# L1 slots and attention's norms emitted in steps, with blocks in between

## Chip, cores and metric

The kernel runs on one core of a Trainium2 chip. The metric is the device time of one launch in microseconds (us). All arithmetic is in 32-bit floats.

## The reference, cut to what matters

2048 tokens of 256 features (two sequences of 1024, seen by the layer-1 attention as they stand) go through two "macaron" layers: half an expert layer, a mixing layer, half an expert layer.

```python
x = x + 0.5 * _L0_ffn_ref(_layernorm(x), ...)   # 8 experts of width 176, top 2, and a shared expert
x = x + _L0_attn_ref(_layernorm(x), ...)        # RWKV time mix and channel mix
x = x + 0.5 * _L0_ffn_ref(_layernorm(x), ...)
x = x + 0.5 * _L1_ffn_ref(_layernorm(x), ...)   # 32 experts of width 96, top 6, and a shared expert
x = x + _L1_attn_ref(_layernorm(x), ...)        # linear attention with rotary turns, no softmax
x = x + 0.5 * _L1_ffn_ref(_layernorm(x), ...)

def _L1_ffn_ref(hidden_states, gate_w, wg, wu, wd, sg, su, sd):
    scores = jax.nn.sigmoid(x @ gate_w)
    topk_w, topk_i = jax.lax.top_k(scores, TOP_K)
    topk_w = topk_w / (jnp.sum(topk_w, axis=-1, keepdims=True) + 1e-20)
    ...
    routed = jnp.einsum('tef,efd,te->td', act, wd, combine)
    shared = jax.nn.silu(hidden_states @ sg) * (hidden_states @ su) @ sd
    return routed + shared

def _L1_attn_ref(X, W_in, b_in, W_out, b_out):
    Q, K, V = jnp.split(jnp.einsum('bsd,ed->bse', X, W_in) + b_in, 3, axis=-1)
    A = jnp.sum(feature_map(K) * V, axis=-2)      # K and Q turned before
    return jnp.einsum('bsd,ed->bse', A[:, None, :] * Q, W_out) + b_out + X
```

## The kernel before

**Names.** The tokens are 16 tiles of 128 in `x`, which stays on the chip. Four tiles are a group (`BT`). Layer 0's second expert layer is `L_0` or m0 (all 16 tiles, four groups); layer 1's are done in passes 0 and 1, each in halves A and B of 8 tiles, so `L_0A`, `L_0B`, `L_1A`, `L_1B`, each with groups g0 and g1. In the profile's names the numbers of groups and buffers are left out.

**An expert layer.** For each group, `measure` normalizes the rows (`normalize`, lines 129 to 147: statistics and the norm on VectorE, a square root and part of the norm on ScalarE, into `xn`, or `axl_at` in pass 1), turns them over on TensorE (psum `pt`, line 156), copies them back on ScalarE (`xT`, line 442), and multiplies them with the router (`lg`, line 456). `choose` finds the top six on VectorE (`taken`, line 202, and the weights). `plan` counts the chosen rows per expert (`count`, line 479), ranks them (`rank`, line 501 ff., and `far`, line 528) and gives each its row number in a table sorted by expert (`idx`, line 567). `scatter` writes the rows to that table in HBM with indirect transfers from GpSimd (`xs_A`, `xs_B`, line 576). Measure, choose and plan together are called the slots of a group.

**Blocks.** The sorted table is worked in blocks of 128 rows (78 for m0; at least 68 and up to 79 for each half of layer 1). A block loads its rows (`xb`), transposes them (`px`, line 755, copied to `xbT` on ScalarE), multiplies with its expert's gate and up weights (`pg`, line 777; `g` on ScalarE, `h` on VectorE), transposes h (`ph`, line 687), multiplies with the down weights (`py`, line 794), copies to `yb` on VectorE (line 802) and stores to `ys`. `combine` gathers each token's six rows (`yk`, indirect transfers from GpSimd, line 814) and adds them into `x` on VectorE (line 826). The shared expert is done by the tile, with the same psum tags. Blocks past the sure number stand behind a condition on the counts (line 919).

**Attention** (`attend`, once per half between the passes): `norms` of a group, then a tile at a time (`tile_of`), then the sum A, and `out_of`, whose products `po` (line 1021) are added into `x` at line 1270. Then follow the slots of pass 1.

**What sets the order.** Each engine does its instructions in the order in which they were emitted, as a scheduler keeps it. `Clock` (line 307) is a planner written by hand: each block runs with `clock.run(us)` for a planned time (`BLOCK`, 2.45 us in layer 0, 1.41 in layer 1), and within it wakes threads that are due: gathers, scatters, slots, attention. `yield clock.spent(us, gap)` says that the part just emitted takes `us` of the blocks' engine time, and is due again `gap` later. What a thread emits under `behind_blocks()` is pinned behind the newest block's last product and yb copy. GpSimd's transfers have one fixed order (`in_turn`), three and then a pause of five memsets; those of `between()` are in one written order: gathers of m0 for groups 0 and 1, scatters of 0A g0, gathers of m0 g2, scatters of 0A g1, gathers of m0 g3, scatters of 0B.

**Where the change lies.** `onward` emits the slots of an L1 group among the blocks of the stage before: first `prep` (measure and choose) in one piece, then `plan` in one. `attend` emits a group's `norms` in one piece, due again after 8.0 us. The slots of 0A and 0B g0 lie among m0's last blocks, those of 0B g1 at the first blocks of 0A, those of 1A among the last of 0B, those of 1B at the end of 0B's shared tiles and the first blocks of 1A.

Of the kernel before, what the change touches and what calls it, by code (L numbers as in the profile page):

```python
# [55 lines left out]
def macaron_kernel(ctx: ExitStack, tc: tile.TileContext, a: dict, out: bass.AP):  # L56
# [12 lines left out]
    def bank(tag, name):  # L69
        return psum.tile([P, TB], F32, tag=tag, name=name)  # L70
# [53 lines left out]
    def statistics(src, n, name):  # L124

        mv = small.tile([P, n, 2], F32, tag="mv", name=f"mv_{name}", bufs=4)
        for i in range(n):
            st = small.tile([P, 6], F32, tag="st", name=f"st_{name}_{i}", bufs=4)
            nc.vector.bn_stats(st, src[i])
            nc.vector.bn_aggr(mv[:, i, :], st)  # L130
        rstd = small.tile([P, n], F32, tag="rstd", name=f"rstd_{name}", bufs=4)
        nc.scalar.activation(rstd, mv[:, :, 1], AF.Sqrt, bias=eps)
        nc.vector.reciprocal(rstd, rstd)
        shift = small.tile([P, n], F32, tag="shift", name=f"shift_{name}", bufs=4)
        nc.vector.scalar_tensor_tensor(shift, mv[:, :, 0], -1.0, rstd, ALU.mult, ALU.mult)
        return rstd, shift

    def normalize(src, dst, n, name):

        rstd, shift = statistics(src, n, name)  # L140
        for i in range(n):
            if i % 2:
                nc.scalar.activation(
                    dst[i], src[i], AF.Identity, bias=shift[:, i : i + 1], scale=rstd[:, i : i + 1]
                )
            else:
                nc.vector.tensor_scalar(
                    dst[i], src[i], rstd[:, i : i + 1], shift[:, i : i + 1], ALU.mult, ALU.add
                )
        return rstd, shift  # L150

    def transposed(src, c, name):

        pt = bank("pt", f"pt_{name}_{c}")
        for i in range(BT):
            nc.tensor.transpose(
                pt[:, i * P : (i + 1) * P], src[i][:, c * P : (c + 1) * P], ident
            )
        return pt
# [216 lines left out]
    clock = Clock()  # L376
# [11 lines left out]
    @contextmanager  # L388
    def behind_blocks():
        with ExitStack() as st:  # L390
            for d in clock.block.values():
                st.enter_context(tc.issue_after(d))
            yield
# [7 lines left out]
    def sparse_moe(layer, w, name, x, xs, ys, moe, given=None, out=None, bufs=2, counts="pt"):  # L401
# [25 lines left out]
        def places(t):  # L427

            h, i = divmod(t, HT)
            if h not in xn:  # L430
                pool = home["pool"]
                xn[h] = pool.tile([P, HT, D], F32, tag="xn", name=f"xn_{name}_{h}", bufs=2)
                xT[h] = pool.tile([P, DC, SEQ], F32, tag="xT", name=f"xTs_{name}_{h}", bufs=2)
            return xn[h], xT[h], i
# [3 lines left out]
        def features_of(b, xb, xbT, o, sub):  # L438

            normalize(x[BT * b : BT * b + BT], xb, BT, sub)  # L440
            for c in range(DC):
                nc.scalar.copy(xbT[:, c, o * P : o * P + TB], transposed(xb, c, sub))

        logits = {}

        def measure(b):
            sub = f"{name}_{b}"
            xb, xbT, o = places(BT * b)
            xb = [xb[:, o + i, :] for i in range(BT)]
            sent[b] = xb  # L450
            features_of(b, xb, xbT, o, sub)
            lg = bank("pt", f"lg_{sub}")[:, 0 : BT * E].rearrange("p (t e) -> p t e", e=E)
            logits[b] = lg
            for i in range(BT):
                for c in range(DC):
                    nc.tensor.matmul(
                        lg[:, i, :],
                        xbT[:, c, (o + i) * P : (o + i + 1) * P],
                        w["router"][:, c, :],
                        start=(c == 0),  # L460
                        stop=(c == DC - 1),
                    )

        def choose(b):
            ts = slice(BT * b, BT * b + BT)
            route(w, logits.pop(b), f"{name}_{b}", taken[:, ts, :], comb[:, ts, :])

        def prep(b):
            measure(b)
            choose(b)  # L470

        def plan(g):


            sub = f"{name}_{g}"
# [21 lines left out]

            pr = bank("py", f"rank_{sub}")[:, 0 : BT * E].rearrange("p (t e) -> p t e", e=E)  # L500
            nc.tensor.matmul(pr, before, taken[:, lo:hi, :], start=True, stop=False)
            for t in range(BT - 1):
# [63 lines left out]
                nc.vector.max(top[:, t, :], slot[:, t, :])  # L566
            nc.vector.tensor_scalar(idx[:, lo:hi, :], top[:, lo:hi, 0:K], -1.0, None, ALU.add)
            groups.append(dict(count=count, cum=cum, open=open_))

        def scatter(g, rank=0):  # L570

            for t in range(BT * g, BT * g + BT):
                for k in range(K):
                    yield from clock.call(rank)
                    with in_turn():
                        d = nc.gpsimd.indirect_dma_start(  # L576
                            out=xs,
                            out_offset=bass.IndirectOffsetOnAxis(
                                ap=idx[:, t, k : k + 1], axis=0
                            ),  # L580
                            in_=sent[g][t - BT * g],
                            in_offset=None,
                        )
                    clock.called(d)
                    tc.declare_no_dep(
                        d.ins, group=f"slots_{name}", reason="a slot is one pair's"
                    )
                    tc.add_to_no_dep_group(f"slots_{name}", d.ins)
                    scattered.append(d.ins)
# [58 lines left out]
        parts = [0] * NT  # L648
# [241 lines left out]
        def blocks(onward=None):  # L890
# [34 lines left out]
        return dict(  # L925
            home=home,
            measure=measure,
            choose=choose,
            prep=prep,
            plan=plan,  # L930
            scatter=scatter,
            owners=owners,
            weights=weights,
# [213 lines left out]
    def wait(done):  # L1147
        while not done():
            yield clock.now + 1.0

    def attend(s, moe, added, result):
# [9 lines left out]
        def norms(g):  # L1161
            ts = slice(g * BT, (g + 1) * BT)
            lg = [xl[:, t, :] for t in range(TPB)][ts]
            rstd, minus[g] = normalize(xs[ts], lg, BT, f"{name}_{g}")
            for c in range(DC):
                nc.scalar.copy(
                    xT[:, c, g * TB : (g + 1) * TB], transposed(lg, c, f"{name}_{g}")
                )

            more = small.tile([P, BT], F32, tag="more", name=f"more_{name}_{g}")  # L1170
            nc.vector.tensor_scalar(more, rstd, 1.0, None, ALU.add)
            for i, xt in enumerate(xs[ts]):
                nc.vector.scalar_tensor_tensor(
                    xt, xt, more[:, i : i + 1], at["b_out"], ALU.mult, ALU.add
                )
# [54 lines left out]

        for g in range(TPB // BT):
            yield from wait(lambda: g in added)
            with behind_blocks():
                norms(g)
            yield clock.now + 8.0
            for t in range(g * BT, (g + 1) * BT):
                with behind_blocks():
                    tile_of(t)
                yield clock.spent(3.0, 4.6)
# [68 lines left out]

    def slots_of(b):
        def slots():  # L1310
            m0["prep"](b)
            m0["plan"](b)
            every_step(m0["scatter"](b))

        return slots
# [9 lines left out]
    def every_step(part):  # L1325
        clock.pool = 0.0
        for _ in part:
            clock.pool = 0.0
# [48 lines left out]
    with ExitStack() as rwkv_stack:  # L1377
# [3 lines left out]
        with tc.tile_pool(name="moe_L0_0", bufs=1) as pool:  # L1381
            m = sparse_moe("L0", w0, "L0_0", x, xs["L0"], ys["L0"], pool, bufs=1, counts="py")
# [24 lines left out]
        for h in range(2):  # L1407
# [7 lines left out]
        rw["pool"] = rwkv_stack.enter_context(tc.tile_pool(name="rwkv", bufs=1))  # L1415
        early_pool = l0_stack.enter_context(tc.tile_pool(name="early", bufs=1, side="right"))
        m0 = sparse_moe(
            "L0",
            w0,
            "L0_1",  # L1420
            x,
            xs["L0"],
            ys["L0"],
            early_pool,
            bufs=1,
# [21 lines left out]
    def half(n, h, **more):  # L1447
# [2 lines left out]
            "L1", w1, f"L1_{n}{k}", x[HT * h : HT * h + HT], xs[k], ys[k], moe_pool, **more  # L1450
        )

    def onward(m, g, planned):

        with behind_blocks():
            m["prep"](g)
        yield clock.spent(6.0, 12.0)

        if g == 0:
            yield from wait(lambda: not planning)  # L1460
            planning.append(m)
        with behind_blocks():
            m["plan"](g)
        yield clock.spent(3.5, 7.0)
        planned.add(g)
        if g == m["groups"] - 1:
            planning.pop()
# [154 lines left out]
```

## Time and profile before

| | |
|---|---|
| runs | 1374.47, 1380.77, 1383.33 us, median 1380.77 |
| profiled execution | 1382.64 us, span 1380.9 us, mean granted TensorE clock 0.913 |
| TensorE busy | 1243.8 us, 90% of the span |
| weight loads, VectorE, ScalarE, GpSimd busy | 965.4, 710.3, 610.7, 660.5 us |
| first L1 slot to the end of 1A's start (562 to 1110 us), TensorE idle in gaps over 0.4 us | 55.8 us |
| GpSimd, indirect transfers | gathers and scatters, about 0.97 us each |

How to read the lines: PE is TensorE, PEld its weight loads, DVE VectorE, ACT ScalarE, POOL GpSimd, SP SyncE. A line of a timeline gives the start in us from the span's start, the length in us, engine, line of the kernel, operation, what it writes and reads, shapes and how many instructions were joined (x8); in square brackets is the idle time of the engine just before, and what ended it. The page's digits are 40 slices of the span, each the busy share in tenths (9 is 90% or more); PEclk is the clock that TensorE was granted, in tenths of full speed.

### The profile page before, as it was taken

The numbers are of one execution on the slowest core, as the hardware profiler recorded it, in microseconds if no ns is written. First come the engines' busy times: TensorE is split into PE (matmuls) and PEld (weight loads), VectorE is DVE, ScalarE is ACT, GpSimd is POOL, SyncE is SP. The second block draws the span as 40 slices with busy tenths as digits, with TensorE's granted clock in tenths as the row PEclk, the third lists the DMA queues.
The fourth block names the chain that finished last, engine by engine and source line by source line (L and its number), as shares of the span: only waits on it lengthen the run. The fifth ranks groups of instructions, "written<-read, shape, count | busy, mean of one in ns | idle before, by whom it ended". The sixth has DMA issues, their size and how long they took to land. (4 is left out here: it accounts for less than half of the span.)

```text
span 1380.9 us, 23073 instructions
## 1 busy us (share of the span) xinstructions
PE 1243.8 (90%) x6100; PEld 965.4 (70%) x6100; DVE 710.3 (51%) x2500; ACT 610.7 (44%) x1660; POOL 660.5 (48%) x1296
## 2 busy tenths in 40 slices
PE   7999999899998899899799998988899789999970
PEld 5767765566676677677579986867655679989850
DVE  5432567644414423554454456764587345456653
ACT  4324475865524133533245555543323155556520
POOL 0620443111113702577777175406667777276475
PEclk9799999999997699999879999997889699999995
DMA  9813434980009224432948685623322258788743
GB/s 284 266 65 108 144 101 133 307 288 1 0 0 243 81 89 126 123 111 92 265 163 269 199 236 175 193 74 103 104 66 77 80 193 265 215 248 265 236 134 105
DMA packets 195171, 214.94 MB, mean 156 GB/s; under 512 B 40893, under 2 KB 178013, under 8 KB 195037
## 3 DMA queue, kind: packets, MB, share of 16 engines
q1 hardware_dynamic: 170460, 146.22, 34.3%
q0 software_dynamic: 24576, 67.14, 15.8%
q8 instruction: 59, 0.97, 0.3%
q14 instruction: 76, 0.61, 0.2%
HBM read 103.04 MB, written 110.23 MB: 154 GB/s over the span
## 5 line engine op out<-in xcount | busy, mean ns | idle before, releaser
L814 POOL DMA_INDIRECT yk_L<-ys_L,idx_L x64 | 61.8, 965 | 174.5 <-DMA ys_L<-yb_L 120.0
L333 POOL MEMSET still<- 128x96 f32 x588 | 105.3, 179 | 33.7
L777 PE MATMUL pg_L_b<-L0gu,xbT_L 128*128 x312 | 108.1, 470 | 1.0 <-ACT xbT_L L759 0.6
L576 POOL DMA_INDIRECT xs_L<-xn_L,idx_L x64 | 61.8, 966 | 78.3 <-DVE taken_L L202 31.4
L670 PE MATMUL pg_L<-L0sgu,xTs_L 128*128 128x352 f32 x256 | 97.7, 516 | 1.7 <-DVE h_L L660 1.3
L814 POOL DMA_INDIRECT yk_L_0B<-ys_B,idx_L_0B x48 | 49.2, 1026 | 72.1 <-DMA xb_L_0B<-xs_B 46.9
L794 PE MATMUL py_L_b<-L0down,hT_L_b 88*128 x312 | 81.3, 382 | 0.0
L814 POOL DMA_INDIRECT yk_L_0A<-ys_A,idx_L_0A x48 | 46.3, 965 | 60.9 <-DMA xb_L_0A<-xs_A 28.7
L660 DVE TENSOR_TENSOR h_L_b<-g_L_b,pg_L_b 128x176 f32<-128x176 f32 x78 | 26.2, 336 | 92.1 <-ACT g_L_b L659 78.8
L794 PEld LDWEIGHTS py_L_b<-L0down,hT_L_b 88*128 88x128 f32 x312 | 58.9, 192 | 19.1 <-issue 0.8
L814 POOL DMA_INDIRECT yk_L_1A<-ys_A,idx_L_1A x48 | 46.8, 975 | 48.0 <-DMA xb_L_1A<-xs_A 23.9
L777 PEld LDWEIGHTS pg_L_b<-L0gu,xbT_L 128*128 128x128 f32 x312 | 55.2, 195 | 20.5 <-DVE h_L_b L660 1.3
L670 PEld LDWEIGHTS pg_L<-L0sgu,xTs_L 128*128 128x128 f32 x256 | 50.6, 212 | 25.5 <-issue 5.9
L777 PE MATMUL pg_L_0B_b<-L1gu,xbT_L_0B 128*128 x272 | 60.8, 351 | 1.3 <-DVEq L919 1.3
L1009 PE MATMUL pkk_cm<-mk_cm,w_WkeyT 128*128 128x512 f32 x128 | 58.7, 594 | 1.5 <-ACT sk_cm L1110 0.9
L777 PE MATMUL pg_L_0A_b<-L1gu,xbT_L_0A 128*128 x272 | 59.3, 343 | 0.8 <-DVE h_L_0A_b L660 0.4
L1021 PE MATMUL pkv_cm<-w_WvalT,sk_cm 128*128 128x256 f32 x256 | 58.6, 379 | 0.1
L814 POOL DMA_INDIRECT yk_L_1B<-ys_B,idx_L_1B x48 | 45.7, 951 | 26.9 <-DMA ys_B<-yb_L_1B 11.7
L1021 PEld LDWEIGHTS pkv_cm<-w_WvalT,sk_cm 128*128 128x128 f32 x256 | 48.3, 190 | 13.7 <-issue 7.2
L777 PE MATMUL pg_L_1A_b<-L1gu,xbT_L_1A 128*128 x272 | 57.3, 334 | 0.3 <-DVE m_L_1B L193 0.2
L777 PE MATMUL pg_L_1B_b<-L1gu,xbT_L_1B 128*128 x272 | 55.7, 327 | 1.3 <-DVEq L919 1.3
L576 POOL DMA_INDIRECT xs_A<-xn_L_0A,idx_L_0A x48 | 46.8, 975 | 18.4 <-issue 13.1
(640 smaller groups left out, 3306.0 us busy)
## 6 DMA issues: line engine op xcount, KB each, us to landing
xs_A<-zero SPq DMA_DIRECT2D x1, 10112.0 KB
xs_B<-zero SPq DMA_DIRECT2D x1, 10112.0 KB
xb_L<-xs_L SPq DMA_DIRECT2D x78, 128.0 KB
ys_L<-yb_L SPq DMA_DIRECT2D x78, 128.0 KB
xb_L_0A<-xs_A SPq DMA_DIRECT2D x68, 128.0 KB
ys_A<-yb_L_0A SPq DMA_DIRECT2D x68, 128.0 KB
xb_L_0B<-xs_B SPq DMA_DIRECT2D x68, 128.0 KB
ys_B<-yb_L_0B SPq DMA_DIRECT2D x68, 128.0 KB
```

Source lines behind the costliest of these rows:

```text
L333: d = nc.gpsimd.memset(still, 0.0)
L576: d = nc.gpsimd.indirect_dma_start(out=xs, out_offset=bass.IndirectOffsetOnAxis(ap=idx[:, t, k : k + 1], axis=0), in_=sent[g][t - BT * g], ...
L660: nc.vector.tensor_tensor(dst, g, pg[:, width : 2 * width], ALU.mult)
L670: nc.tensor.matmul(pg, xbT[:, c, i * P : (i + 1) * P], w["sgu"][:, c, u, :, :].rearrange("p z w -> p (z w)"), start=(c == 0), stop=(c == D ...
L777: nc.tensor.matmul(pg, xbT[:, c, :], w["gu"][:, c, bass.ds(e, 1), :, :].rearrange("p e z h -> p (e z h)"), start=(c == 0), stop=(c == DC - 1),
L794: mm = nc.tensor.matmul(py, hT[0:HP, k, :], w["down"][:, bass.ds(e, 1), k, :].rearrange("p e d -> p (e d)"), start=(k == 0), stop=(k == C ...
L814: d = nc.gpsimd.indirect_dma_start(out=yk, out_offset=None, in_=ys[0 : n * P, :], in_offset=bass.IndirectOffsetOnAxis(ap=idx[:, t, k : k + ...
L1009: nc.tensor.matmul(ps, w[:, c, oc * P : (oc + 1) * P], src[:, c, :], start=(c == 0), stop=(c == DC - 1),)
L1021: nc.tensor.matmul(ps, src[:, c, i * P : (i + 1) * P], w[:, c, :], start=(c == 0), stop=(c == n - 1),)
```

## The change

A slot of layer 1 is emitted in four pieces instead of two: norms; transposes, logits and choice; counts; ranks. Attention's norms are emitted in two pieces: the norm itself; transposes and the rest. Each piece is pinned behind the newest block (`in_steps`, `behind_blocks`). The planned times of a slot sum to the same as before, 6.0 and 3.5 us, with gaps of 12 and 7 us, and 8.0 us for the norms. The slots of layer 0 (`slots_of`) keep their order.

```diff
--- before.py
+++ after.py
@@ -438,17 +438,22 @@
         def features_of(b, xb, xbT, o, sub):
 
             normalize(x[BT * b : BT * b + BT], xb, BT, sub)
+            yield 1.5, 5.5
             for c in range(DC):
                 nc.scalar.copy(xbT[:, c, o * P : o * P + TB], transposed(xb, c, sub))
 
         logits = {}
 
         def measure(b):
+            for _ in measure_steps(b):
+                pass
+
+        def measure_steps(b):
             sub = f"{name}_{b}"
             xb, xbT, o = places(BT * b)
             xb = [xb[:, o + i, :] for i in range(BT)]
             sent[b] = xb
-            features_of(b, xb, xbT, o, sub)
+            yield from features_of(b, xb, xbT, o, sub)
             lg = bank("pt", f"lg_{sub}")[:, 0 : BT * E].rearrange("p (t e) -> p t e", e=E)
             logits[b] = lg
             for i in range(BT):
@@ -465,11 +470,16 @@
             ts = slice(BT * b, BT * b + BT)
             route(w, logits.pop(b), f"{name}_{b}", taken[:, ts, :], comb[:, ts, :])
 
-        def prep(b):
-            measure(b)
+        def prep_steps(b):
+            yield from measure_steps(b)
             choose(b)
+            yield 4.5, 6.5
 
         def plan(g):
+            for _ in plan_steps(g):
+                pass
+
+        def plan_steps(g):
 
 
             sub = f"{name}_{g}"
@@ -497,6 +507,7 @@
 
 
 
+            yield 1.5, 2.0
             pr = bank("py", f"rank_{sub}")[:, 0 : BT * E].rearrange("p (t e) -> p t e", e=E)
             nc.tensor.matmul(pr, before, taken[:, lo:hi, :], start=True, stop=False)
             for t in range(BT - 1):
@@ -566,6 +577,7 @@
                 nc.vector.max(top[:, t, :], slot[:, t, :])
             nc.vector.tensor_scalar(idx[:, lo:hi, :], top[:, lo:hi, 0:K], -1.0, None, ALU.add)
             groups.append(dict(count=count, cum=cum, open=open_))
+            yield 2.0, 5.0
 
         def scatter(g, rank=0):
 
@@ -926,8 +938,9 @@
             home=home,
             measure=measure,
             choose=choose,
-            prep=prep,
+            prep_steps=prep_steps,
             plan=plan,
+            plan_steps=plan_steps,
             scatter=scatter,
             owners=owners,
             weights=weights,
@@ -1162,6 +1175,7 @@
             ts = slice(g * BT, (g + 1) * BT)
             lg = [xl[:, t, :] for t in range(TPB)][ts]
             rstd, minus[g] = normalize(xs[ts], lg, BT, f"{name}_{g}")
+            yield
             for c in range(DC):
                 nc.scalar.copy(
                     xT[:, c, g * TB : (g + 1) * TB], transposed(lg, c, f"{name}_{g}")
@@ -1230,9 +1244,13 @@
 
         for g in range(TPB // BT):
             yield from wait(lambda: g in added)
+            parts = norms(g)
             with behind_blocks():
-                norms(g)
-            yield clock.now + 8.0
+                next(parts)
+            yield clock.now + 5.5
+            with behind_blocks():
+                next(parts, None)
+            yield clock.now + 2.5
             for t in range(g * BT, (g + 1) * BT):
                 with behind_blocks():
                     tile_of(t)
@@ -1308,7 +1326,8 @@
 
     def slots_of(b):
         def slots():
-            m0["prep"](b)
+            m0["measure"](b)
+            m0["choose"](b)
             m0["plan"](b)
             every_step(m0["scatter"](b))
 
@@ -1450,18 +1469,23 @@
             "L1", w1, f"L1_{n}{k}", x[HT * h : HT * h + HT], xs[k], ys[k], moe_pool, **more
         )
 
+    def in_steps(parts):
+
+        while True:
+            with behind_blocks():
+                cost = next(parts, None)
+            if cost is None:
+                break
+            yield clock.spent(*cost)
+
     def onward(m, g, planned):
 
-        with behind_blocks():
-            m["prep"](g)
-        yield clock.spent(6.0, 12.0)
+        yield from in_steps(m["prep_steps"](g))
 
         if g == 0:
             yield from wait(lambda: not planning)
             planning.append(m)
-        with behind_blocks():
-            m["plan"](g)
-        yield clock.spent(3.5, 7.0)
+        yield from in_steps(m["plan_steps"](g))
         planned.add(g)
         if g == m["groups"] - 1:
             planning.pop()
```

## The prediction

> **What bounds the kernel now.** I read the page first, then the PE timeline from 540 to 1115 us with the idle time ahead of each instruction, then POOL's, DVE's and ACT's timelines around each place that the change touches, and last the chain of waits. The page says that TensorE is the bound, with one light stretch in slices 17 to 32:
>
> ```profile
> PE 1243.8 (90%) x6100; PEld 965.4 (70%) x6100; DVE 710.3 (51%) x2500; ACT 610.7 (44%) x1660; POOL 660.5 (48%) x1296
> PE   7999999899998899899799998988899789999970
> POOL 0620443111113702577777175406667777276475
> PEclk9799999999997699999879999997889699999995
> ```
>
> A slice is 34.5 us. Where PE falls to 7 or 8, PEclk falls too. The L1 slots and attention's norms lie there. The PE timeline shows one such place (slots of 1A, first and second group):
>
> ```profile
> 948.43 0.70 PE L794 MATMUL py_L_0B_b<-L1down,hT_L_0B_b 96*128 x2
> 954.96 1.97 PE L156 MATMUL pt_L_1A<-ident,axl_at 128*128 128x128 f32 x8 [5.83 <-DVE axl_at L147]
> 957.39 3.69 PE L456 MATMUL lg_L_1A<-L1router,axT_at 128*128 128x32 f32 x16 [0.46 <-ACT axT_at L442]
> 960.89 1.01 PE L687 MATMUL ph_L_0B_b<-ident,h_L_0B_b 128*96 128x128 f32 x2
> ...
> 967.43 0.41 PE L479 MATMUL count_L_1A<-ones,taken_L_1A 128*32 128x1 f32 x8
> ...
> 988.67 1.97 PE L156 MATMUL pt_L_1A<-ident,axl_at 128*128 128x128 f32 x8 [3.60 <-DVE axl_at L147]
> ```
>
> PE stands still until the norm is done, transposes, takes the logits, and then has 6.5 us of block work (960.89 to 967.43) before the counts. So today the transposes wait and the counts don't. The same waits ahead of transposes elsewhere: 0A g0 1.68 + 0.66 us (562.6), 0A g1 0.87 + 1.45 (584.6), attention of pass 0 2.08 (841.9) and 3.37 (898.4), 1A g0 5.83 + 0.46, 1A g1 3.60 + 0.46, attention of pass 1 1.52 (1050.4), 1B g0 2.44. They sum to 24.4 us: the most that direct waiting can give back.
>
> The second bound is POOL, which moves all rows of the routed experts in one order fixed by hand:
>
> ```profile
> 573.85 0.95 POOL L814 DMA_INDIRECT yk_L<-ys_L,idx_L  x1 [0.30 <-issue]
> 581.24 1.01 POOL L576 DMA_INDIRECT xs_A<-xn_L_0A,idx_L_0A  x1 [5.31 <-DVE idx_L_0A L567]
> ...
> 1000.27 0.97 POOL L814 DMA_INDIRECT yk_L_0B<-ys_B,idx_L_0B  x1 [4.68 <-DVE x L721]
> ```
>
> After 581.24 POOL has no gap until 764, and from 936.6 to 1106 it waits only 4.68 us and less than 5 more. Pass 1A begins at 1109.52 after a PE wait of 4.96 us for rows that POOL's last scatter (1104.87) brought. So between 936 and 1109 a PE wait counts only if it holds up a POOL transfer.
>
> **The change, part by part.** The same matrix products, copies and transfers are issued; the planned time is the same too (1.5 + 4.5 = 6.0 and 1.5 + 2.0 = 3.5 us of blocks per slot, 5.5 + 2.5 = 8.0 per norm). Only the order moves, and two activation table loads are added. Nothing ahead of the first L1 slot (562 us) changes, nor the tail after 1324.
>
> *Transposes behind a block.* About one block (1.45 us in L1, 2.45 in L0) now runs on PE between norm and transposes. Gain: up to that much of each wait.
>
> *Counts lose their cover.* Blocks that stood between logits and counts now stand before the transposes. By the new order, 0A keeps only a px, 0B g1 nothing, 1A g0 a ph and a pg pair, 1A g1 and 1B g1 a few small products. The bare way from logits to counts is in the trace where nothing covers it: at 1B g0 lg ends at 1092.35 and the counts start at 1094.49, 2.14 us. I price the new waits at 2.2, 2.2, 2.2, 1.3, 1.2 and 0.7 us for 0A g0, 0A g1, 0B g1, 1A g0, 1A g1, 1B g1: +9.8 us in all on PE. Hiding them would take 2.2 us of block work that the new order does not offer.
>
> *DVE's order.* Splitting lets the gathers' adds of x (L826) in front of the slot's small operations, and DVE waits there for the landing:
>
> ```profile
> 953.89 0.48 DVE L826 SCALAR_TENSOR_TENSOR x<-yk_L_0B,wk_L_0B,x 128x256 f32<-128x256 f32 x1 [1.55 <-DMA yk_L_0B<-ys_B,idx_L_0B]
> 954.48 0.74 DVE L147 TENSOR_SCALAR axl_at<-x,rstd_L_1A,shift_L_1A 128x256 f32<-128x256 f32 x2
> ...
> 957.35 0.95 POOL L814 DMA_INDIRECT yk_L_0B<-ys_B,idx_L_0B  x1 [0.30 <-issue]
> ```
>
> Before, the norm's last step stands behind the add of a gather issued at 950.5. After, for 1A g0, three more adds stand ahead of it, among them that of the gather of 957.35, which lands some 3 us later: transposes at about 961.4 instead of 954.96. The moved blocks fill 4.9 of these 6.4 us, so the wait becomes about 7.4 instead of 5.83. With 1.3 at the counts the slot numbers come near 974.5, where POOL wants them at 973.9 (the scatter moves ahead of one gather): +0.6 on POOL. At 0A g0, the adds of the gathers of 571 to 574 stand ahead of the choice (before: behind it), the counts come near 577 instead of 575.69, and the numbers near 584.9 instead of 580.96: POOL's first scatter is 3.9 us later.
>
> *Sums by place.* (1) 0A and 0B slots. Everything on POOL up to 764 is 3.9 us late. Rows of 0A are not needed before 682, some 3 us after that, and SyncE holds the loads back for other tables anyway (PE waits of 6.10 and 2.79 us at 674.7 and 682.8). But the last gather of L0 delays the add at 688.66, thus 0B g1's transposes (693.41) by 3.9. PE fills this with the shared ph and py and one pg pair, 4.0 us, that stood behind the logits; then the counts wait 2.2. Counts before at 701.31; after 697.3 + 1.15 + 0.6 + 2.23 + 2.2, near 703.6 to 704: +2.7. The PE gains at 0A g0 (2.3) vanish into the 2.2 at its counts, and so at g1 (2.3 against 2.2). Ends: −4.7 (waits vanish, POOL on time) and +6.1 (3.9 + 2.2, nothing fills). I take +2.7.
>
> (2) Attention of pass 0. These waits lie ahead of 936.59, where POOL's full stretch begins, so they count whole. g0 gets 4 us of block work ahead of its transposes, but ACT puts a table load, a g and an xbT copy (1.28 + 0.25 + 0.37) ahead of its share of the norm; g1's square root stands behind another block's g, its last step behind a yb copy. I take 0.75 each: −1.5; ends 0 and −5.45 (both waits gone).
>
> (3) 1A slots and the end of 0B. In the new order 0B's last block stands ahead of 1A g1's transposes: its end comes 6.4 us earlier, 990.3. POOL still has 12 scatters queued, which end at 996.5: its 4.68 us at 1000.27 shrink by 3.8. Ends: −4.7 (wait gone) and +6 (numbers of 1A g0 late by the whole 6.4, POOL waits with everything behind it). I take −3.8 + 0.6 = −3.2.
>
> (4) Attention of pass 1 on PE: some +2.9 us (two table loads and a g on ACT ahead of the copies), covered by the 4.96 us wait at 1104.57; without that cover it would be paid. I take 0.
>
> (5) 1B g1 among PE-bound blocks: +0.7; ends 0 and +2.2.
>
> *Table loads.* The row, with what follows on ACT:
>
> ```profile
> 841.42 1.28 ACT L132 ACT_TABLE_LOAD   x1
> 842.72 0.30 ACT L132 ACTIVATE rstd_at<-mv_at,eps 128x4 f32<-128x4 f32 x1
> ```
>
> Two more cost ACT 2.6 us, inside (4). The Trainium skill ("ScalarE: Activation LUTs", What ACT_TABLE_LOAD costs) speaks against interleaving other functions: it counts a switch at about 2.66 us, 1283 ns of load and as much again of drain. The 1283 agree with this row, the drain does not show here, since the next ACTIVATE starts 0.02 us after the load; by the page the two would cost 5.3 us and (4) might show through at the 1A start, by the row they stay under it.
>
> *Clock.* In the window 949 to 972, which starts with the 5.83 us wait, the granted clock is 0.70, and 0.85 in 563 to 570 after waits of 1.68 and 0.66. Waits of 2 us in all were thus enough before; I keep the clock as it is and leave its change to the range. The Trainium skill ("TensorE: Matmul & The Clock Gate", Part 1) puts the throttle at an idle window of about 3.4 us; by it the places with 2.2 us would run at full clock, which would give a few us more. The row at 563 does not agree.
>
> Sum: 2.7 − 1.5 − 3.2 + 0 + 0.7 = −1.3, rounded with half-clock pieces that get shorter at 1A g1 to −2 us. The profiled execution took 1382.64 us, span 1380.9 and 1.7 around it; the median of the runs, 1380.77, lies 1.9 below. Set against the median: 1379 us.
>
> **The rivals.** (a) *Waits vanish.* The moved blocks cover the norms, counts are hidden by what DVE finishes sooner. For it: each norm chain is short, and 46.87 us of POOL idle before 936.59 would carry a gain on. Against: the 2.14 us at 1092.35. −4.7 (0A) −5.45 (attention) −4.7 (POOL at 1000): −14.8, about 1366 us. Chance 0.19.
>
> (b) *POOL late.* Adds of x ahead of the slot's operations on DVE make the numbers late, and POOL, in order, holds every later transfer. For it: the 5.31 us wait at 581.24 is of this kind. Against: POOL's 4.68 us at 1000.27 can absorb as much. Price 6.1 in (1) and 6 in (3), with 0.7: +13, about 1394 us. It decides once the 1A g0 numbers come over 5 us after 973.9. Chance 0.20.
>
> (c) *The change does not do what it says.* With planned time unchanged, waits only change name, transposes to counts, place by place: 0 to +1, 1381 us. Chance 0.11. It differs from the forecast in 0B's end, which stays at 1000.
>
> **How the numbers follow.** The forecast, 1379, has 0.50; its own range is 1373 to 1386 (ends of (2), half of those of (1) and (3)). The range 1364 to 1393 reaches to (a) and (b). One per cent is 13.8 us, about what a measurement can tell from no change: below 1367 lies 0.18 (most of (a)), above 1394.6 lies 0.18 (half of (b) and unknown clock loss), between them 0.64.
>
> **What would show it.** Right: idle time of 1 to 2.5 us "<-DVE taken" ahead of the counts at 0A, 0B g1 and 1A; 5 to 8 us still ahead of 1A g0's transposes; the first 0A scatter some 4 us later after its gathers; POOL's wait at the end of 0B under 2 us; the 1A start within 5 us of 1109. Wrong: no count waits (a), or a POOL wait over 5 us for 1A's numbers (b), or PE idle between 540 and 1110 away from its 56 us by more than 8.

## The result and the profile after

The changed kernel takes 1392.32 us (median of 20 runs, 1382.46 to 1398.85), the kernel before 1380.09 us (20 runs, 1370.76 to 1390.97). The ratio is 1.0081, with a 95% interval of 1.0056 to 1.0105: slower by 0.8%, some 11 us. The profiled execution has a span of 1391.0 us and a mean granted clock of 0.908.

From the page of the changed kernel, the same four lines as before:

```profile
PE 1244.7 (89%) x6100; PEld 966.2 (69%) x6100; DVE 711.8 (51%) x2500; ACT 617.8 (44%) x1662; POOL 664.1 (48%) x1296
PE   7999999899997899799789999987998799999970
POOL 1520534111114603377777175407777777166475
PEclk9899999999997699899879999996889589999995
```

PE's busy time is nearly the same in sum (1244.7 us against 1243.8), so most of the 10 us more of span is time in which it waited; within single stages the busy time moves with the clock, as shown below. In the PEclk line four slices are lower by a tenth (from 556, 939, 1078 and 1113 us on), and the second is higher by one.

To see where the time went, I took the start of the same instruction in both traces and subtracted the shift that the two have where their order is still equal (product 231 of layer 0's blocks, 548.2 us before, 546.1 after: −2.1 us, which belongs to the execution and not to the change).

| start of | before | later after the change, shift taken off | of it in this stage | forecast |
|---|---|---|---|---|
| last product of layer 0's shared expert | 655.4 | +9.0 | +9.0 | |
| 131st block transpose of 0A | 794.0 | +12.6 | +3.6 | +2.7 for both |
| 17th product of attention's `pqk` | 910.2 | +2.8 | −9.8 | |
| POOL's first gather of 0B | 936.6 | +6.3 | +3.5 | −1.5 for both |
| first block transpose of 1A | 1109.5 | +5.1 | −1.2 | −3.2 |
| 131st block transpose of 1A | 1209.1 | +9.5 | +4.4 | +0.7 |
| end | 1380.9 | +12.3 | +2.8 | 0 |

The last column is the prediction's term for the stage.

The loss is at 0A's slots. PE's timeline there, and 60 us later among the shared products:

```profile
568.59 0.42 PE L767 MATMUL px_L<-ident,xb_L 128*128 128x128 f32 x2
576.16 0.58 PE L489 MATMUL count_L_0A<-ones,taken_L_0A 128*32 128x1 f32 x8 [7.16 <-DVE taken_L_0A L202]
...
638.58 0.94 PE L699 MATMUL ph_L<-ident,h_L 128*128 128x128 f32 x3 [2.99 <-DVE h_L L672]
```

The waits ahead of 0A g0's transposes are gone (they were 1.68 and 0.66 us), and one of 7.16 us stands ahead of its counts. DVE's timeline says what `taken`, the result of the choice, waited for:

```profile
573.34 0.48 DVE L838 SCALAR_TENSOR_TENSOR x<-yk_L,wk_L,x 128x256 f32<-128x256 f32 x1 [1.27 <-DMA yk_L<-ys_L,idx_L]
573.75 0.46 DVE L193 MAX8 m_L_0A<-s_L_0A 128x8 f32<-128x32 f32 x4
...
575.88 0.23 DVE L202 TENSOR_SCALAR taken_L_0A<-rest_L_0A 128x128 f32<-128x128 f32 x1
...
636.45 0.48 DVE L838 SCALAR_TENSOR_TENSOR x<-yk_L,wk_L,x 128x256 f32<-128x256 f32 x1 [8.09 <-DMA yk_L<-ys_L,idx_L]
```

The logits end at 568.75. Six adds of x, each waiting for a gather to land, stand on DVE between 564.5 and 573.8 ahead of the choice (MAX8); before, it was one. So `taken` ends 7.4 us after the logits; before, it was 2.5. POOL's timeline shows the numbers' lateness:

```profile
587.44 1.01 POOL L588 DMA_INDIRECT xs_A<-xn_L_0A,idx_L_0A  x1 [12.16 <-DVE idx_L_0A L578]
```

The first scatter starts at 587.44, 8.3 us later than before when the shift is taken off (the prediction had 3.9). It holds up the gathers behind it: at 636.45 an add on DVE waits 8.09 us for one of them, an `h` stands behind the add, and PE waits 2.99 us for that `h`. The windows give the clock, 546 to 627 (layer 0's blocks with 0A's slots) and 852 to 870 (attention's first norm) of the changed kernel:

```profile
546.00:627.00 81.00, 71.17 (x351) 53.49 (x350) 43.52 (x174) 33.95 (x81) 47.23 (x101) 0.89 0.35 113
...
852.00:870.00 18.00, 15.36 (x73) 10.83 (x73) 14.10 (x43) 9.54 (x28) 8.13 (x17) 1.00 0.45 142
```

and the one that answers to the second, before:

```profile
842.00:860.00 18.00, 14.92 (x59) 10.96 (x60) 10.68 (x35) 8.98 (x24) 5.00 (x12) 0.81 0.41 130
```

The number after the five engines is the granted clock. At attention it rose from 0.81 to 1.00. The norms' waits there on PE are shorter (2.08 and 3.37 us before):

```profile
855.58 0.44 PE L156 MATMUL pt_at<-ident,axl_at 128*128 128x128 f32 x2 [1.14 <-ACT axl_at L143]
...
907.92 1.09 PE L156 MATMUL pt_at<-ident,axl_at 128*128 128x128 f32 x8 [1.38 <-DVE axl_at L147]
```

At 1A g0 the wait is longer, as forecast:

```profile
965.42 1.97 PE L156 MATMUL pt_L_1A<-ident,axl_at 128*128 128x128 f32 x8 [7.92 <-DVE axl_at L147]
```

### The profile page after: what moved, and what is told of

It is laid out like the page before. It is cut to its first block, busy times and chain, and to the rows that moved or that the text cites. A ratio compares the mean times of both kernels' runs of the same rounds, so it can differ in the third digit from the quotient of the medians.

```text
span 1391.0 us, 23120 instructions
## 1 busy us (share of the span) xinstructions
PE 1244.7 (89%) x6100; PEld 966.2 (69%) x6100; DVE 711.8 (51%) x2500; ACT 617.8 (44%) x1662; POOL 664.1 (48%) x1296
## 5 line engine op out<-in xcount | busy, mean ns | idle before, releaser
L789 PE MATMUL pg_L_0B_b<-L1gu,xbT_L_0B 128*128 x272 | 57.2, 335 | 1.2 <-DVEq L931 0.7
```

The source lines that it names most:

```text
L789: nc.tensor.matmul(pg, xbT[:, c, :], w["gu"][:, c, bass.ds(e, 1), :, :].rearrange("p e z h -> p (e z h)"), start=(c == 0), stop=(c == DC - 1),
```

## The experiments

Theory A: at 0A's first slot the adds of x get ahead of the choice on DVE; the choice comes late, and with it PE's counts and POOL's scatters. Theory B: the counts lost the blocks that covered them, at all six places alike. Theory C: chance in the granted clock. The kernels ran on several chips, on which the kernel before takes 1380 to 1420 us, so ratios to the kernel before on the same chip are compared, each with its 95% interval, and positions in the traces only relative to the shift named above. A trace is one execution; runs of one kernel scatter with a standard deviation of some 5 us, the furthest 10 us from the median.

### Which slots

The change taken apart: a slot that isn't in steps is emitted as before.

```diff
-        yield from in_steps(m["prep_steps"](g))
+        stepped = f"{m['name']}" in SPLIT or f"{m['name']}_{g}" in SPLIT
+        if stepped:
+            yield from in_steps(m["prep_steps"](g))
+        else:
+            with behind_blocks():
+                for _ in m["prep_steps"](g):
+                    pass
+            yield clock.spent(6.0, 12.0)
```

(and in the same way for `plan_steps`; `SPLIT` lists the halves in steps). All in steps but 0A:

> Only the two slots of 0A are put back into one piece each (6.0 and 3.5 us of planned time, as before the change); all else stays split. Theory A (0A's first slot: the adds of x get ahead of its choice on DVE, POOL's scatters start late, and the lateness travels to 0A's start): this kernel loses the delay at 562 to 716 us and keeps what attention gains, so 1374 to 1380 us against 1380 of before, some 12 us under the changed kernel. Theory B (the counts lost their cover at all six places alike): only two of six places are mended, so about 1388. Theory C (chance in the granted clock): 1390 as the changed kernel.

Only 0A, attention's norms whole:

> The kernel before with only the two slots of 0A emitted in steps; the other slots and attention's norms in one piece. Theory A: the whole delay up to 716 us appears here, +9 to +13 us, so 1389 to 1393 us, with 0A's first block some 9 us later than before and everything after it shifted evenly. Theory B: two of the six count waits, +3, about 1383. Theory C: within 3 us of before.

Only attention's norms:

> Attention's norms in two pieces, all slots in one piece as before. Nothing before 836 us moves. Theory A: the gain of some 5 us that the trace of the changed kernel shows between 840 and 860 us stays, of which POOL's full stretch passes on most: 1375 to 1378 us, a little faster than before. Theory B says nothing on it, the prediction's own term was -1.5: 1379. Were attention's split a loss, it would be over 1382.

All slots, attention's norms whole:

> All L1 slots in steps, attention's norms in one piece. Theory A: the changed kernel without its one gain, 1394 to 1398 us. Theory B: about 1391. If the norms' split were itself a part of the loss, it would come out under 1390.

| kernel | ratio | interval |
|---|---|---|
| all but 0A | 1.0026 | 0.9997 to 1.0056 |
| only 0A | 1.0097 | 1.0062 to 1.0132 |
| only attention's norms | 0.9977 | 0.9946 to 1.0008 |
| all slots, norms whole | 1.0074 | 1.0045 to 1.0103 |

0A's two slots alone cost as much as the whole change. Theory A's place is right; theory C had the kernel with only 0A within 3 us of before, and it is 16 us above. Theory A's sizes were less good: all but 0A was expected at 0.996 to 1.000 and came out at 1.0026 (its interval reaches just under 1), so the other slots may cost a little, and all slots with the norms whole was expected at 1.010 to 1.013 and came out at 1.0074, where theory B had put it (1391 us, 1.008). So in these times the norms' split gains little. Alone it gains 0.2%, not clear of its interval, though both traces with it show PE some 9 to 10 us sooner between 844 and 910 us and neither without it does. In the kernel with only 0A the wait is nearly the same:

```profile
584.60 0.59 PE L489 MATMUL count_L_0A<-ones,taken_L_0A 128*32 128x1 f32 x8 [6.53 <-DVE taken_L_0A L202]
```

and its window over layer 0's last blocks, the same work as 548 to 626 before (78 us at a clock of 0.91):

```profile
555.00:642.00 87.00, 77.80 (x349) 57.45 (x348) 44.17 (x174) 33.77 (x80) 50.86 (x109) 0.80 0.34 108
```

### Which split, and whether the adds are the cause

Only the second half of 0A's slots in two pieces (counts, ranks):

> The kernel before, but the slots of 0A have only their second half (counts, ranks) in two pieces; norm to choice stay one piece. In DVE's order the choice then still stands behind one add of x, as before. Theory A (adds of x ahead of the choice): ratio to before 1.000, within 0.3%, no count wait over 1 us. Rival B2 (pinning the ranks behind a block of 2.45 us delays the slot numbers): POOL's first scatter 2.5 to 5 us late and about +0.5%.

Only the first half in pieces:

> The kernel before, with the slots of 0A split in front of the transposes and behind the choice, and the counts and ranks in one piece. Five adds of x stand ahead of the choice, as the norm's split makes it. Theory A: nearly the whole loss of the 0A split, ratio 1.007 to 1.010, a count wait of 4 us or more at 0A g0. Rival B2 (the ranks' pinning): 1.003 or less.

0A as in the change, but the adds of x for m0's group 1 emitted later:

```diff
-        def combine(g, rank=0, lag=4):
+        def combine(g, rank=0, lag=4, flush=0.8):
...
-                yield clock.now + 0.8
+                yield clock.now + flush
...
-        yield from given_rows(m0, (0, 1), added0)
+        yield from given_rows(m0, (0,), added0)
+        yield from wait(lambda: 1 in m0["ready"])
+        yield clock.now + 3.0
+        yield from m0["combine"](1, 0, 7, 2.4)
+        added0.add(1)
```

> The slots of 0A in steps exactly as in the kernel with only 0A split (ratio 1.0097), but the adds of x for m0's group 1 are emitted later (eight gathers ahead of the first add instead of five, 2.4 us between the last ones), so that two adds instead of six stand ahead of the choice on DVE. Theory A: the wait at 0A g0's counts falls from 6.5 us to 2 to 3 us, the first scatter of 0A comes 3 to 4 us sooner after its gathers, and the ratio falls to 1.000 to 1.004. Theory B (moved block work, lost cover): nothing changes, 1.008 to 1.011. If POOL is not the way on which the delay goes but PE's own wait is, the gain is still some 4 us here.

The three ran on one chip. The first was 1.0030 (1.0007 to 1.0054), with no wait at the counts of 0A and the first scatter 2.9 us late, so the ranks' pinning is not free, but small. The second was 1.0066 (1.0036 to 1.0097), with a wait of 3.79 us at 0A g0's counts, slightly under the range that theory A gave. The third was 0.9975 (0.9949 to 1.0001), against 1.0097 on another chip: the loss is gone, by more than theory A gave (1.000 to 1.004), and the wait at the counts is the bare way from logits to counts:

```profile
584.13 0.59 PE L489 MATMUL count_L_0A<-ones,taken_L_0A 128*32 128x1 f32 x8 [1.82 <-DVE taken_L_0A L202]
```

The traces agree on the size: from the end of 0A g0's logits to the end of `taken` it takes 6.7 to 7.4 us in the four traces with six adds between norm and choice, 4.0 with five, 3.7 to 3.8 with four, 2.0 to 2.1 with two and 2.3 to 2.5 with one. The adds' place on DVE is thus shown as the cause of the late choice, and with it of the loss at 0A. What the later adds are worth without 0A's steps was not run. The kernel with late adds does not yet tell which way the delay travels, since in it both PE's wait and POOL's lateness went.

### The cover of the counts

0A whole, the others in steps, the counts due later:

```diff
-            yield 4.5, 6.5
+            yield 4.5, 12.0
```

> Attention's norms in two pieces; slots of 0B, 1A and 1B in steps, but the counts due 12 us after the choice instead of 6.5, so that blocks stand between logits and counts again; 0A in one piece. With the short gap this was 1.0026. If the waits at the counts (2.2, 0.8, 2.3 us and less in the trace) are what the other slots' split costs: 0.998 or lower, level with attention alone (0.9977), and no wait at the counts of 0B g1 and 1B g1. If later numbers hold POOL up instead: 1.003 to 1.008, with longer POOL waits ahead of 1A's scatters.

It measured 0.9922 (0.9901 to 0.9943). Then the same number changed in the full changed kernel, with and without late adds, and at single places:

> The changed kernel with one number changed: the counts of every L1 slot are due 12 us after the choice instead of 6.5. At 0A g0 four adds of x still stand ahead of the choice on DVE, but three blocks now stand between logits and counts on PE. If 0A's loss is PE's own wait at the counts (7.16 us in the changed kernel), it is covered and the ratio falls to about 0.990 to 0.995. If it is POOL's late start (theory A: numbers late whatever PE does meanwhile), 0A stays late by 8 us or more and the ratio is 0.998 to 1.004, between the 0.992 of the kernel with 0A whole and the changed kernel's 1.008.

> Everything split; adds of x for m0's group 1 late (two ahead of the choice); counts of 0B, 1A and 1B due after 12 us, of 0A after 6.5. By the two cures measured alone (0.9975 against 1.0097 at 0A, 0.9922 with 0A whole) the ratio should be 0.988 to 0.993. If the two overlap, that is, if what 0A gains only lengthens a wait at its end, it stays at 0.992 to 0.996.

> As the kernel with 0A whole, norms split and long gap (0.9922), but the long gap for 0B's slots alone; 1A and 1B have the short one. The traces put most of the difference between 1.0026 and 0.9922 at the start of 0A, where 0B g1 has its counts: if so, 0.992 to 0.995. If the cover counts at 1A and 1B as much, 0.996 to 1.000.

> Everything split, adds of x late and counts due after 12 us everywhere, 0A too. One add of x ahead of the choice and three blocks ahead of 0A's counts. No count wait at 0A, slot numbers of 0A g0 some 3 us later than with the short gap. If PE is the bound there, it beats the kernel with the short gap at 0A, 0.985 to 0.990; if POOL is, it is level or worse, 0.990 to 0.995.

| kernel | ratio | interval |
|---|---|---|
| changed kernel, counts after 12 us everywhere | 0.9909 | 0.9878 to 0.9941 |
| adds late; 12 us at 0B, 1A, 1B | 0.9891 | 0.9850 to 0.9933 |
| 0A whole; 12 us at 0B alone | 1.0031 | 1.0000 to 1.0061 |
| adds late; 12 us everywhere | 0.9899 | 0.9859 to 0.9940 |

The gap at 0B alone gives nothing, less than either expectation. With late adds the long gap at 0A too is level with the short one. One number, 6.5 or 12, takes the changed kernel from 1.008 to 0.991 (on different chips). I had expected 0.998 to 1.004 if POOL's late start were the way of 0A's loss. So the way had to be measured by itself, in the kernel before with only 0A in steps and the long gap there, beside a kernel with the long gap at 1A and 1B alone, and the changed kernel again:

> The kernel before with only 0A's slots in steps, and their counts due 12 us after the choice. Four adds of x still stand ahead of the choice and POOL's first scatter still comes some 5 us late; only PE has blocks to do meanwhile. If 0A's loss is PE's wait with the half clock after it: ratio 0.994 to 1.001, against 1.0097 with the short gap. If it is POOL's lateness: 1.005 or more.

> 0A whole, attention's norms split, 0B with the short gap, 1A and 1B with the long gap. The same with the short gap everywhere gave 1.0026, with the long gap at 0B alone 1.0031, at 0B, 1A and 1B 0.9922. If 1A and 1B carry the gain of the cover: 0.993 to 0.996. If it takes both places together: 0.997 to 1.001.

> The changed kernel itself, once more beside the others on the same chip: 1.0081 again, within 0.4%. Its trace decides whether the delay of 9 us at the end of layer 0 and the shorter attention repeat; a second trace also shows whether the half clock at the turn from 1A to 1B (2 to 3 us) was chance: then it is absent here or also in the other traces.

The first: 1.0023 (0.9995 to 1.0051), against 1.0097 with the short gap. Its timelines of PE and POOL:

```profile
575.98 0.41 PE L489 MATMUL count_L_0A<-ones,taken_L_0A 128*32 128x1 f32 x8
...
584.29 1.01 POOL L588 DMA_INDIRECT xs_A<-xn_L_0A,idx_L_0A  x1 [8.66 <-DVE idx_L_0A L578]
```

PE has no wait at the counts, and POOL starts 3.6 us later than before (shift taken off), after waiting 8.66 us. The ratio lies between the two expectations (up to 1.001 and from 1.005). The long gap did not take off PE's wait alone: four adds instead of six stand ahead of the choice, and POOL's lateness fell from 8.8 us to 3.6 us. So 0.7% of 0A's 1.0% went with PE's wait, the half clock behind it and more than half of POOL's lateness together. That PE's wait is the larger part is argued, not shown: in the kernel with only the first half in pieces the first scatter is 1.5 us late only, PE waits 3.79 and 1.80 us at 0A's counts, and the ratio is 1.0066, against 0.9975 with the late adds on the same chip. The second, 1.0033 (1.0009 to 1.0056), fell outside both expectations. The changed kernel again: 1.0077 (1.0047 to 1.0106). Its trace has the wait at 0A g0's counts again (6.99 us), layer 0's end 7.9 us late, PE's gain at attention (−8.1 us from the 131st block transpose of 0A to the 17th `pqk`, −9.8 in the first trace), and at the turn from 1A to 1B a clock of 0.88 over 14 us where the first trace has 0.76 and the kernel before 1.00.

That the long gap gave 1.003 at 0B alone, 1.003 at 1A and 1B alone, and 0.992 at both could belong to the chips. Long and short gap with 0A whole, and the best kernel, on one chip:

> The kernel with 0A whole, attention's norms split and the long gap at 0B, 1A and 1B, again (0.9922 on a chip where the kernel before takes 1420 us). With the long gap at 0B alone or at 1A and 1B alone it was 1.003. If the two places work only together or the gain is real: 0.990 to 0.995 again. If the first measurement owed something to its chip: 0.996 to 1.002, about what the parts give.

> The same with the short gap everywhere (1.0026 on a chip where the kernel before takes 1412 us), beside the one with the long gap on one chip. The gap's whole worth at 0B, 1A and 1B is the difference: 1.0% by the first measurements, 0.3% or less if the chips differed.

> All slots in steps, adds of x late, long gap at 0B, 1A and 1B (0.9891 before). Again 0.985 to 0.993, and below the kernel with 0A whole by 0.3% to 0.6%, since 0A's steps end layer 0 some 8 us sooner when neither the adds nor the counts hold PE up.

Long gap 0.9976 (0.9952 to 0.9999), short gap 1.0004 (0.9977 to 1.0031), all in steps with late adds and the long gap 0.9842 (0.9811 to 0.9874; 0.985 to 0.993 was expected). The first 0.9922 does not repeat: away from 0A the gap is worth some 0.3%, 4 us, where the waits forecast at those four counts sum to 5.4 us. Why each place alone gave 1.003 stays open; effects of that size are not told apart by these intervals. 0A's steps and the late adds together are worth 1.3% on this chip (0.9842 against 0.9976, more than the 0.3% to 0.6% expected); with the adds ahead of the choice the same steps cost 1.0%. How the 1.3% divides between the steps and the adds was not measured.

That last kernel is faster than the kernel before on two chips: 1366.08 us against 1380.7, and 1391.4 against 1411.16.

## Why the prediction was wrong, step by step

It said 1379 us and no change; the time is 1392, slower by less than 1%. Rival (b) had the sign and, at 1394, nearly the time. None of the prediction's three signs of being wrong came: counts did wait, POOL waited at most 2.49 us at 1A's numbers, and PE's idle time in gaps over 0.4 us, from 540 us to 1A's start, rose from 55.8 to 63.0 us, by less than 8. The signs looked at idle time and not at the clock.

**Term (1), 0A and 0B: forecast +2.7, measured +12.6. This step failed.** The way was followed rightly as far as the counts: 577 was forecast for their start, 578.3 measured (shift taken off). But the wait ahead of them was priced at 2.2 us, the bare way from logits to counts, though the same working had the counts held back by adds of x. The logits end at 570.9 in the trace (shift taken off); set against this end, the forecast start of the counts would have made 577 − 570.9 = 6.1 us. The two halves of the term were worked out side by side and never put on one time line. Measured: 7.16 us, and 6.5 to 7.0 in the other three traces with this order. POOL's first scatter, forecast 3.9 us late, came 8.3 us late. The waits at the other counts were nearer: 1.82 at 0A g1 and 2.28 at 0B g1 (2.2 forecast), 0.82 at 1A g1 (1.2), none at 1A g0 (1.3) and 1B g1 (0.7).

The second part of the failure is the clock, which the prediction kept as it was. Layer 0's last blocks with 0A's slots, the same products in each kernel, take 78 us at a clock of 0.91 before. With waits of 6.5 to 7.2 us at 0A g0's counts they take 86 to 87 us at 0.80 in three traces (only 0A, all slots with the norms whole, the changed kernel again), but 81 us at 0.89 in the first trace of the changed kernel, shown above: the same waits do not cost the same clock in every execution. In the kernel with late adds and long gap, which has no wait there:

```profile
551.00:617.00 66.00, 65.80 (x351) 49.77 (x350) 35.20 (x146) 34.16 (x80) 41.89 (x89) 1.00 0.41 131
```

It is 66 us at 1.00. From 66 to 87, in the kernel with only 0A, are 21 us, of which waiting makes some 9 (6.53 and 1.80 and 0.64); the other 12 are the same products at the lower clock (PE busy 77.80 us against 65.80). In the first trace of the changed kernel it is 15 us, with waits of 9.4. In the kernel with only 0A and late adds, waits of 1.82 and 0.50 us stand there, and the window has a clock of 0.95 over 70 us, against 1.00 without a wait. The Trainium skill ("TensorE: Matmul & The Clock Gate", Part 1) puts the throttle after an idle window of about 3.4 us. The measurement decides, as the row at 563 did: waits shorter than that did cost clock here.

**The way to 0A's start.** The prediction saw POOL's delay meet PE at the last gather of layer 0 (688.66). It met it earlier, at 636.45: the gathers of group 2, then an add on DVE, an `h` behind it, 2.99 us on PE and a clock of 0.87 from 627 to 653. PE's own lateness and POOL's look like two ways to the same end, of which the later one decides: in the first trace layer 0's blocks end 2.9 us late and the shared products add 6.1; in the traces with only 0A and of the changed kernel again, the blocks end some 8 to 9 us late and the shared products add nothing.

**Term (2), attention: forecast −1.5, measured −9.8 on PE, −6.3 where POOL's full stretch begins.** The sign was right, the size not even inside the bound of −5.45, which was made of waits alone. The waits fell by 2.9 us in sum; the clock, 0.81 in two windows of 18 us before (6.8 us lost), is 1.00 and 0.89 after (1.8 us lost in 16). 2.9 and 5.0 are 7.9 of the 9.8.

**Term (3), 1A and the end of 0B: forecast −3.2, measured −1.2.** Transposes of 1A g0 after 7.92 us (7.4 forecast), POOL without a wait at 0B's end (0.30 us at 1003.02), and POOL waits of 2.49 us (ended on DVE by `slot_L_1A`, a step to 1A's numbers) and 0.98 us at 1A's first scatter, where 0.6 was forecast.

**Terms (4) and (5).** 1A starts after a PE wait of 3.16 us for POOL's rows, so what PE lost to the added table loads stayed covered, as forecast. At 1B g1 +4.4 instead of +0.7: the clock is 0.79 in 1112 to 1145, 0.93 in 1110 to 1140 before. The 2.8 us after 1209 are mostly a lower clock at the turn to 1B (0.76 over 14 us, 1.00 before), where PE waits 2.6 us in all after the change and 2.2 before. How much of it was chance stays open: the second trace of the changed kernel has a clock of 0.88 there and loses about 2 us from 1209 to the end.

**The rivals.** (b) was right in kind, adds of x ahead of a slot's operations, and in time. It was wrong in place, since 1A's numbers cost little, and it left out PE's wait. That its time came near is luck: it is the sum of 6.1 at 0A and 6 at 1A, where +12.6 and −1.2 were measured; the rest of the measured +12.3 comes from attention (−6.3), which it left out, and from 1A's start on (+7.2), priced at 0.7. (a) needed the counts to be hidden; with one number changed those at 0A and 0B are, and then the kernel takes 0.9909, 1368 us, close to the 1366 that (a) named.

## What to carry to other kernels

When a chain of small steps is cut into pieces among other work, write down for each cut what will stand between the pieces on every in-order queue it uses, and put all queues on one time line: a wait is the arrival of one less the arrival of the other, never a fixed latency. The cover taken from one wait must be paid back at the next, here by making the counts due later, and a step that others wait for must not stand behind adds that wait for transfers. Price a PE wait with the clock behind it, and as a range: here waits of 9 us cost 15 us in one execution and 21 in another.

## What the runs showed of the hardware that I had not expected

The granted clock over the same 350 products was 1.00 where no wait was over 0.14 us, 0.95 with waits of 1.82 and 0.50 us, 0.91 with five waits of 0.46 to 1.68 us (5.1 us in all, the kernel before), and 0.80 with waits of 6.53, 1.80 and 0.64 us: a series of short waits cost clock as well as a long one. But the same waits cost different amounts: the same five gave 0.93 in the kernel with only attention's norms split, and 7.16 and 1.82 us gave 0.89 in one trace of the changed kernel, 6.99 and 1.82 us 0.80 in the other. Chips differ: the kernel before took 1380 us on some and 1411 to 1420 us on others, and a ratio of 0.9922 measured on one came back as 0.9976 on another; differences under half a per cent need kernels side by side on one chip.
